# The last 65 keys of an attention kernel: queries become the stationary operand, VectorE turns the scores in blocks and ScalarE places them; the next x is read three groups later

## The chip, the cores and the metric

The kernel runs on one core of a Trainium2 chip. The time is the device time of one execution in microseconds (us). Before the change the median of three runs is 2532.07 us (2532.05 to 2533.65). The engines are PE (TensorE, with PEld for its weight loads), DVE (VectorE), ACT (ScalarE), POOL (GpSimd) and SP (SyncE, here only a DMA queue). A line such as L1246 is line 1246 of the kernel before the change.

## The reference

A gated cross-attention block followed by a mixture-of-experts layer, all in float32:

```python
# x (4, 256, 512), ctx_4096 (4, 1601, 512); 32 query heads, 8 key/value heads, head size 128
def attn(query, kv):                        # Wq (512, 4096), Wkv (512, 2048), Wo (4096, 512)
    q = (query @ Wq + bq).reshape(B, L, NKV, G, HDIM)            # G = 4 query heads share a key head
    k_, v_ = jnp.split(kv @ Wkv + bkv, 2, axis=-1)
    k, v = k_.reshape(B, Lk, NKV, HDIM), v_.reshape(B, Lk, NKV, HDIM)
    scores = jnp.einsum('blkgd,bmkd->bkglm', q, k) * scale
    a = jax.nn.softmax(scores, axis=-1)
    o = jnp.einsum('bkglm,bmkd->blkgd', a, v).reshape(B, L, NHEAD * HDIM)
    return o @ Wo + bo

x = x + tanh(g_xattn) * attn(layernorm(x), ctx_4096)
x = x + tanh(g_ffn) * moe(layernorm(x))     # a base matrix and 8 low-rank experts, the top 2 of them used
```

There are 1601 keys: twelve tiles of 128 and a rest of 65.

## The kernel before

**Groups.** Attention is done in 64 groups: 4 sequences `b`, 8 key heads `h`, 2 row blocks `l` of 128 queries. In one group the 4 query heads that share a key head lie side by side, so a group has W = 4 x 128 = 512 columns (query head, query). A group's scores are held with the keys on partitions: one tile `p` is 128 x 2 x 512, for a pair of key tiles. `pairs` begins with the rest alone (`(FULL,)`, unit j = 0), then six pairs of full tiles (j = 1 to 6).

**Scores** (`score_unit`, L1217 to L1261). For each key tile one float32 matmul: the keys `kT` (128 head dimensions x 128 keys, or x 65 for the rest) are the stationary operand, the 512 query columns of `qT` move, and the result lies in one PSUM bank with the keys on partitions. For the rest this is 65 partitions x 512. ScalarE copies the bank into the tile `p` (L1255). From unit j = 2 on, VectorE folds the tiles into a running maximum (`fold`, L1168 to L1181). The first fold, at j = 2, takes the pairs 1 and 2 and also the rest.

**Softmax and the second product.** `softmax` (L1268) finishes the maximum over the keys (five steps on VectorE, two of them block transposes), and queues for each unit a subtraction on VectorE (L1285), an exponential on ScalarE (L1288) and a sum on VectorE. `av_unit` (L1321 to L1337) multiplies with the values, `v` stationary. `run_group` (L1783) goes through the units of the current group and does the av units of the group before one step behind: scores j, then av j - 1. After a group `window` (L1800) puts in projections for the coming heads (q, k and v, in seven half-size products instead of eight, lines 1004 and 1015) and the output product (L472).

**What sets the order.** The instructions of TensorE, VectorE and ScalarE are issued in an order that a planner in the kernel's Python works out while it is traced. It keeps a clock for each engine: `spend(ns)` moves TensorE's clock on, `vec(ns)` and `act(ns)` those of VectorE and ScalarE, with durations that are written in the code. Work that may come later is put in queues (`later`), among them `sub`, `exp`, `ln` (layer norms), `sum` and `norm`. `pump` issues from the heads of the queues whatever can begin by the planner's clock, and in a tie the `sub` queue goes first. `fit("v", t)` issues queued work that fits before time `t`. `force(key)` issues a piece that is needed now. `Task`s hold TensorE steps with a due group. `short_tasks` (L1749) puts in steps of at most 432 ns between the units. On the chip each engine then runs its own instructions in this order and waits for semaphores. PSUM has 8 banks, given out by `bank` and given back by `give`.

**The next x.** Queries are projected for two sequences at once (`JOINT` = 2), so x is read twice: for sequences 0 and 1 at the start, for 2 and 3 in the middle. The second reading is started in the loop over groups, at (b, h, l) = (1, 4, 1), that is group 25, counting from 0:

```python
            if (h, l) == (NKV - 4, 1) and b + 1 < B and (b + 1) % JOINT == 0:
                load_pair("q", b + 1, 0)
                tasks.append(Task(x_steps(b + 1), now + 7))
```

`load_pair` issues on SP the load of the first query weights, kept in DRAM with their sums (896 KB). `x_steps` (L589) then issues: two loads of x tiles on SP (256 KB each), the bias `bo` on POOL; for each of four tiles a layer norm (VectorE statistics, a ScalarE square root, VectorE scaling), four transposes on TensorE with a VectorE copy out, a VectorE addition of the bias, two 128 KB stores on POOL and, for the first two, the load of one more tile on SP; at the end four VectorE differences (L653). The query projection of sequence 2, `pxq`, begins in the window after group (1, 7, 0) is scored, group 30.

Of the kernel before, what the change touches and what calls it, by code (L numbers as in the profile page):

```python
# [15 lines left out]
P = 128  # L16
NHEAD = 32
NKV = 8
HDIM = 128
G = NHEAD // NKV  # L20
# [7 lines left out]
def flamingo_kernel(  # L28
# [51 lines left out]
    nc = tc.nc  # L80
    B, L, D = x.shape
# [7 lines left out]
    FULL = KT - 1 if rows[-1] < P else KT  # L89
# [4 lines left out]
    pairs = [tuple(range(i, min(i + 2, FULL))) for i in range(0, FULL, 2)]  # L94
# [6 lines left out]
    HK = FULL // 2 * P  # L101
    NSUB = -(-HK // 512)
    SUB = HK // NSUB
    REST = rows[-1] if FULL < KT else 0
# [13 lines left out]
    SEM = 200  # L118
# [3 lines left out]
    clock = {"now": 0.0, "v": 0.0, "a": 0.0, "hold": 0.0}  # L122
    free = [0.0] * NBANK
    done = {}
    queues = {q: deque() for q in ("sub", "oT", "so", "exp", "ln", "T", "norm", "turn", "sum", "low", "low_a")}

    def vec(ns, ready=None):

        clock["v"] = max(clock["v"], clock["now"] + SEM if ready is None else ready) + ns
        return clock["v"] + SEM  # L130

    def act(ns, ready=None):
        clock["a"] = max(clock["a"], clock["now"] + SEM if ready is None else ready) + ns
        return clock["a"] + SEM
# [5 lines left out]
    def start_of(piece):  # L140
        engine, _, ready, _, _ = piece
        if not isinstance(ready, float):
            ready = done.get(ready, NEVER)
        return max(clock[engine], ready)

    def take(q):

        piece = q.popleft()
        engine, ns, _, fn, key = piece
        start = start_of(piece)  # L150
        fn()
        clock[engine] = start + ns
        if key is not None:
            done[key] = start + ns + SEM + (GP_COPIES if False else 0)

    def pump(until=NEVER, most=None):

        n = 0
        while most is None or n < most:
            heads = [(start_of(q[0]), i, q) for i, q in enumerate(queues.values()) if q]  # L160
            if not heads:
                return n
            start, _, q = min(heads)
            if start == NEVER or start + min(q[0][1], 1200) / 2 > until:
                return n
            take(q)
            n += 1
        return n
# [24 lines left out]
    def fit(engine, until):  # L193

        while True:
            some = [
                (start_of(q[0]), i, q)
                for i, q in enumerate(queues.values())
                if q and q[0][0] == engine and start_of(q[0]) + q[0][1] <= until + FIT
            ]  # L200
            if not some:
                return
            take(min(some)[2])

    def spend(ns, ready=0.0):

        clock["now"] = max(clock["now"], ready) + ns
        pump(clock["now"])
        turn_more()

    def bank(name):
        free.remove(min(free))
        return ps.tile([P, 512], F32, tag="bank", name=name)

    give = free.append
# [32 lines left out]
    def mm_cost(n):  # L248

        return 2 * (max(n, P) / 1.2 + 2)  # L250
# [126 lines left out]
    def by_blocks(b, h):  # L377
        return (b, h) not in heads[-2:]
# [206 lines left out]
    JOINT = 2  # L585
# [79 lines left out]
    def key_col(i):  # L665

        return HK if i == FULL else i * P + (REST if i * P >= HK else 0)
# [198 lines left out]
    qT_t, kT_t, v_t = {}, {}, {}  # L866
# [7 lines left out]
    def load_q(b, h):  # L874
        new_q(b, h)
        for g in range(0, G, 2):
            nc.sync.dma_start(qT_t[b, h][:, g : g + 2, :], q_kept[b, h, g])
# [339 lines left out]
    def score_unit(key, j):  # L1217

        b, h, l = key
        nm = "_".join(map(str, key))  # L1220
        free_p = 0.0
        if j == 0:
            p_t[key] = []
            acc_t[key] = pool.tile([P, 2, W], F32, tag="mx", name=f"mx_{nm}", bufs=1)
        if key == last and j > 0:

            if j == 1:
                flat = pool.tile([P, NC * 2 * HW], F32, tag="ctxT", name="p_last", bufs=1)
                late.extend(
                    flat[:, i * 2 * W : (i + 1) * 2 * W].rearrange("p (t w) -> p t w", t=2)  # L1230
                    for i in range(NPAIR - 1)
                )
            p = late.pop(0)
        else:

            if len(ring) >= NBUF:
                before, i = ring[-NBUF]
                free_p = force(("sum", before, max(i, min(NPAIR - FULL // 2 + 1, NPAIR - 1))))
            ring.append((key, j))
            p = pool.tile([P, 2, W], F32, tag="p", name=f"p_{nm}_{j}", bufs=NBUF)  # L1240
        p_t[key].append(p)
        for k, i in enumerate(pairs[j]):
            r = rows[i]
            spend(mm_cost(W), max(min(free), done.get(("qT", b, h), 0.0)))
            sc = bank(f"sc_{nm}_{i}")
            nc.tensor.matmul(  # L1246
                sc[:r, :],
                kT_t[b, h][:, key_col(i) : key_col(i) + r],
                qT_t[b, h][:, :, l * P : (l + 1) * P],
                start=True,  # L1250
                stop=True,
            )
            t = max(clock["now"] + SEM, free_p)
            fit("a", t)
            nc.scalar.copy(p[:r, k, :], sc[:r, :])  # L1255
            t = act(585, t)
            give(t)
        fit("v", t)
        ns = fold(acc_t[key], ALU.max, j, key)
        if ns:  # L1260
            vec(ns, t)  # L1261

    acc_t, sum_t, late, ring = {}, {}, [], []
    last = (B - 1, NKV - 1, NL - 1)
# [437 lines left out]
    tasks = []  # L1702
# [164 lines left out]
    def next_pair(b, hp):  # L1867
        return (b, hp + 1) if hp + 1 < NKV // 2 else (b + 1, 0) if b + 1 < B else None
# [107 lines left out]
    for hi, (b, h) in enumerate(heads):  # L1976
        pair, coming = (b, h // 2), next_pair(b, h // 2)
        nxt = heads[hi + 1] if hi + 1 < len(heads) else None
        for l in range(NL):
            now = hi * NL + l  # L1980
            cur = (b, h, l)
            if cur == last:
                break
            if (h, l) == (NKV - 4, 1) and b + 1 < B and (b + 1) % JOINT == 0:
                load_pair("q", b + 1, 0)
                tasks.append(Task(x_steps(b + 1), now + 7))
            swap_at["group"] = now
            run_group(cur, prev)
            if prev is not None:
                steps = out_steps(prev)  # L1990
                if steps:
                    tasks.insert(0, Task(steps, now + 1 if by_blocks(*prev[:2]) else None))
                    if by_blocks(*prev[:2]):
                        out_task[prev[:2]] = tasks[0]
            prev = cur
            if (b, h, l) == (B - 1, NKV - 3, NL - 1):
                tail_space()
                tasks.append(Task(ffn_weight_steps() + [(0, 0, early_norms)]))
                both = [ffn_steps(*t) for t in early]
                tasks[:0] = [Task(route, now + 4) for route, _ in both]  # L2000
                tasks.extend(Task(steps, spare=True) for _, steps in both)
            if nxt is not None and nxt[0] % JOINT == 0:
                tasks.append(Task(q_steps(*nxt, l), now, first=True))
            elif nxt is not None and l == 0:
                load_q(*nxt)
            if coming is not None and (h % 2, l) == (0, 1):
                cb, cp = coming
                if cb == b:
                    then = lambda c=coming: next_weights("v", *c)
                    steps = sum(pair_steps("k", cb, cp, then), [])  # L2010
                else:
                    steps = first_k_steps(cb)
                tasks.append(Task(steps, (hi | 1) * NL + (NL - 1) * (cb == b), now))
            if coming is not None and (h % 2, l) == (1, 0):
                cb, cp = coming
                follow = next_pair(cb, cp)
                then = None if follow is None else lambda f=follow: next_weights("k", *f)
                for part in pair_steps("v", cb, cp, then):
                    tasks.append(Task(part, (hi | 1) * NL + NL, now))
                if cb == b and cp == NKV // 2 - 1 and b + 1 < B:  # L2020
                    tasks.append(Task(ctx_steps(b + 1)))
            if (h, l) == (NKV - 1, NL - 1) and b + 1 < B:

                force(("T", "kv", b + 1))
                force(("w", "v", b + 1, 0))
            window(now)
            if l == NL - 1 and nxt == heads[-1]:
                load_wo(*nxt)
# [51 lines left out]
```

## Time and profile before

| | us |
|---|---|
| median of three runs | 2532.07 |
| the profiled execution | 2532.2 |
| its span, first to last instruction | 2530.4 |
| PE busy | 2521.6 |
| PEld busy | 1493.8 |
| DVE busy | 2175.3 |
| ACT busy | 1263.6 |
| POOL busy | 208.8 |

The TensorE clock granted in the records is 1.000 throughout. The largest groups of TensorE are the scores (L1246, 775.9 us in 1664 instructions) and the av products (L1337, 765.5 us in 1664). One float32 matmul is two instructions, each with its own weight load (LDWEIGHTS), so 13 key tiles x 64 groups x 2 make the 1664. ScalarE's copies of the scores (L1255) are 820 of 65 and 128 partitions in a mixed row, 586 ns each. A group takes 39.5 us on average (2530.4 / 64).

How to read the rows. A row of the groups has line, engine, operation, the tiles written and read, the shape and the count, then busy time in all and the mean duration of one in ns, then the idle time of the engine just before them. For a matmul the shape is stationary rows * columns, then the moving partitions x columns. Since TensorE overlaps its instructions, the duration of one is longer than the distance to the next: what an instruction takes from the engine is read from starts in the timeline. A row of the timeline has the start, the length of a run of like instructions, engine, line, tiles, shape and count. In a row of stretches (A:B) the columns are the stretch, its length, the busy time and in brackets the number of instructions, the granted clock, the share of the DMA engines and GB/s.

### The profile page before, as it was taken

Reading aid. Unit: us, or ns where it says so; the run is one execution under the profiler, and the core shown is the slowest. Engines: PE = TensorE matmul, PEld = TensorE weight load, DVE = VectorE, ACT = ScalarE, POOL = GpSimd, SP = SyncE. Lnnn points to the kernel's source line nnn. Section 1 sums busy time; section 2 is a strip of 40 time slices with the busy share of each in tenths; the row PEclk is TensorE's granted clock in tenths of the full one; section 3 lists DMA queues with packets and bytes.
Section 4 is the critical chain, followed back from the end, with each engine's and each line's share of the span. In section 5 each row is a group of like instructions: output and inputs, shape, how many; then the busy total and the mean of one; then the engine's idle time right before and its main releaser. Section 6 shows DMA issues by size and latency. Waiting matters only on the chain.

```text
span 2530.4 us, 27018 instructions
## 1 busy us (share of the span) xinstructions
PE 2521.6 (100%) x9199; PEld 1493.8 (59%) x9199; DVE 2175.3 (86%) x3323; ACT 1263.6 (50%) x2062; POOL 208.8 (8%) x271
## 2 busy tenths in 40 slices
PE   9999999999999999999999999999999999999999
PEld 7557566565555656555665565756656565555544
DVE  4999898898899989999878887878788888889886
ACT  2545454545455554555545454545455455555551
POOL 1000000001001000110010000000000100000100
PEclk9999999999999999999999999999999999999999
DMA  5646857669666543224255535455532222221211
GB/s 170 143 92 130 146 123 118 151 110 246 80 92 99 85 81 74 71 71 152 58 98 100 98 77 96 109 81 110 154 80 65 82 54 67 67 63 44 71 34 50
DMA packets 300136, 246.24 MB, mean 97 GB/s; under 512 B 180533, under 2 KB 256341, under 8 KB 296158
## 3 DMA queue, kind: packets, MB, share of 16 engines
q1 hardware_dynamic: 267278, 211.71, 36.6%
q0 software_dynamic: 32192, 32.55, 8.8%
q8 instruction: 72, 1.18, 0.2%
q14 instruction: 66, 0.54, 0.1%
q10 hardware_dynamic: 528, 0.26, 0.0%
HBM read 147.96 MB, written 96.49 MB: 97 GB/s over the span
## 4 chain that ended last, share of the span: by engine, by line
PE 98%; DVE 1%; DMA 0%; ACT 0%; issue 0%; SPq 0%; ACTq 0%
PE sc L1246 28%; PE av L1337 27%; PE pxv L1015 6%; PE pxk L1004 6%; PE pxq L1004 4%; PE pox L472 4%; PE pyv L1015 3%; PE pyk L1004 3%; PE pyq L1004 2%; PE poy L472 2%; PE pzv L1015 2%; PE pzk L1004 2%; PE pzq L1004 1%; PE ptv L1128 1%; PE poz L472 1%; PE py L1581 1%
## 5 line engine op out<-in xcount | busy, mean ns | idle before, releaser
L1246 PE MATMUL sc<-qT,kT 128*128 128x512 f32 (+1 forms) x1664 | 775.9, 592 | 0.0
L1337 PE MATMUL av<-p,v 65*128 65x512 f32 x1640 | 765.5, 592 | 0.5 <-ACT p L1288 0.5
L1255 ACT COPY p<-sc 65x512 f32<-65x512 f32 x820 | 478.4, 586 | 572.8 <-PE sc L1246 549.0
L1337 PEld LDWEIGHTS av<-p,v 65*128 65x128 f32 x1640 | 311.2, 190 | 384.3 <-issue 380.1
L1246 PEld LDWEIGHTS sc<-qT,kT 128*128 128x128 f32 (+1 forms) x1664 | 308.1, 186 | 375.6 <-issue 349.5
L1285 DVE TENSOR_TENSOR p<-p,mb 65x512 f32<-65x512 f32 x442 | 482.4, 1136 | 0.3
L1288 ACT ACTIVATE p<-p 65x512 f32<-65x512 f32 x442 | 422.3, 990 | 31.0 <-DVE p L1285 29.7
L1181 DVE TENSOR_TENSOR mx<-mx,p 128x1024 f32<-128x1024 f32 x252 | 308.1, 1223 | 146.3 <-ACT p L1255 141.7
L478 POOL DMA_DIRECT2D kept_x<-po x210 | 182.6, 925 | 2039.8 <-ACT po L477 1864.4
L1181 DVE TENSOR_TENSOR sm<-sm,p 128x1024 f32<-128x1024 f32 x252 | 307.6, 1221 | 42.0 <-ACT p L1288 32.0
L1004 PE MATMUL pxq<-xq,wq 128*128 128x256 f32 x512 | 131.2, 379 | 0.0
L1049 ACT ACTIVATE kT<-pxk,biasT 128x384 f32<-128x384 f32 (+1 forms) x120 | 58.1, 509 | 126.5 <-PE pxk L1004 126.0
L1004 PEld LDWEIGHTS pxq<-xq,wq 128*128 128x128 f32 x512 | 92.4, 189 | 32.1 <-issue 15.8
L1049 ACT ACTIVATE qT<-pxq,biasT 128x256 f32<-128x256 f32 x64 | 30.4, 474 | 148.8 <-PE pxq L1004 148.8
L1175 DVE TENSOR_TENSOR mx<-p,p 128x1024 f32<-128x1024 f32 x63 | 76.9, 1221 | 31.6 <-ACT p L1255 31.4
L1004 PE MATMUL pxk<-T,wk 128*128 128x417 f32 (+1 forms) x240 | 90.4, 499 | 0.0
L1015 PE MATMUL pxv<-wv,ctxT 128*128 128x128 f32 x720 | 90.2, 275 | 0.0
L1015 PE MATMUL pxv<-wv,T 128*128 128x128 f32 x720 | 90.2, 275 | 0.0
L1004 PE MATMUL pxk<-ctxT,wk 128*128 128x417 f32 (+1 forms) x240 | 90.0, 499 | 0.0
L1015 PEld LDWEIGHTS pxv<-wv,ctxT 128*128 128x128 f32 x720 | 86.4, 192 | 4.2 <-issue 3.8
L1015 PEld LDWEIGHTS pxv<-wv,T 128*128 128x128 f32 x720 | 86.4, 192 | 4.2 <-issue 3.8
L1052 ACT COPY v<-pxv 128x384 f32<-128x384 f32 x90 | 43.0, 478 | 83.4 <-PE pxv L1015 83.1
(273 smaller groups left out, 2779.5 us busy)
## 6 DMA issues: line engine op xcount, KB each, us to landing
kept_x<-po POOLq DMA_DIRECT2D x210, 128.0 KB, 4.8
wo<-kept_wo SPq DMA_DIRECT2D x22, 1024.0 KB, 7.8
kept_q<-wq SPq DMA_DIRECT2D x16, 896.0 KB, 4.3
wq<-kept_q SPq DMA_DIRECT2D x16, 896.0 KB, 5.1
space<-kept_wo SPq DMA_DIRECT2D x22, 512.0 KB, 3.9
wk<-kept_k SPq DMA_DIRECT2D x11, 896.0 KB, 4.8
wv<-kept_v SPq DMA_DIRECT2D x11, 896.0 KB, 4.6
ctxT<-kept_ctx SPq DMA_DIRECT2D x12, 801.0 KB, 11.8
```

Of the source, the lines that this page charges most:

```text
L472: nc.tensor.matmul(bk[:, :HD], left[i]()[:, c, :], blk[:, c, :], start=first and c == 0, stop=c == 1, skip_group_check=True,)
L478: nc.gpsimd.dma_start(x2_kept[b, l, d], part, accum_op=ALU.add)
L1004: nc.tensor.matmul(bk[:, :n], a(SLOT[i], c), operand(i, c, s, n), start=first and c == 0, stop=c == 1, skip_group_check=True,)
L1015: nc.tensor.matmul(bk[:, t * HDIM : (t + 1) * HDIM], operand(i, c, s + t * P, P), a(SLOT[i], c), start=first and t == 0 and c == 0, stop=c ...
L1049: nc.scalar.activation(dst, src, AF.Identity, bias=bias_of(kind, h0 + f))
L1175: nc.vector.tensor_tensor(acc, p[first], p[first + 1], op)
L1181: nc.vector.tensor_tensor(acc, acc, p[j], op)
L1246: nc.tensor.matmul(sc[:r, :], kT_t[b, h][:, key_col(i) : key_col(i) + r], qT_t[b, h][:, :, l * P : (l + 1) * P], start=True, stop=True,)
L1255: nc.scalar.copy(p[:r, k, :], sc[:r, :])
L1285: nc.vector.tensor_tensor(p, p, m, ALU.subtract)
L1288: nc.scalar.activation(p, p, AF.Exp, scale=scale)
L1337: nc.tensor.matmul(av, v_t[b, h][:r, i, :], p_t[key][j][:r, k, :], start=(j == 0 and k == 0), stop=(j == NPAIR - 1 and k == len(pairs[j]) ...
```

## The change

For the rest of 65 keys `score_unit` now calls a new function, `score_rest`. The 128 queries of each of the 4 query heads are the stationary operand (`qT`, 128 x 128), and the 65 keys move. This makes 4 float32 matmuls, side by side in one bank: queries on partitions, (query head, key) in 4 x 65 columns. VectorE then turns the result in blocks of 32 x 32, out of PSUM into the unused second half of the same tile `p`: one block transpose of 4 x 64 columns, and one of 4 x 32 columns in which the 65th key is repeated 32 times. A block transpose leaves each 32 x 32 block in its place among the partitions, so ScalarE moves the blocks to where they belong: 8 copies of 32 partitions x (4 x 32), and 4 copies of one partition x (4 x 32) for the 65th key. These 12 copies are issued in unit j = 1, behind the two copies of the first pair of full tiles, before the fold. The planner is told 8 x 62 ns for TensorE, 600 ns for VectorE and 12 x 220 ns for ScalarE, in place of 857 ns for TensorE and 585 ns for ScalarE.

The second reading of x starts at group (1, 6, 0), number 28, in place of 25, and is due 3 groups later in place of 7.

```diff
@@ score_unit @@
         p_t[key].append(p)
+        if pairs[j] == (FULL,):
+            score_rest(key, p, free_p)
+            return
         for k, i in enumerate(pairs[j]):
...
             nc.scalar.copy(p[:r, k, :], sc[:r, :])
             t = act(585, t)
             give(t)
+        if key in turned:
+            t = turned.pop(key)(t)
         fit("v", t)
...
+    turned = {}
+
+    def score_rest(key, p, free_p):
+
+        b, h, l = key
+        assert REST == 65
+        spend(G * 2 * 62, max(min(free), done.get(("qT", b, h), 0.0)))
+        sc = bank(f"sr_{'_'.join(map(str, key))}")
+        for g in range(G):
+            nc.tensor.matmul(
+                sc[:, g * REST : (g + 1) * REST],
+                qT_t[b, h][:, g, l * P : (l + 1) * P],
+                kT_t[b, h][:, HK : HK + REST],
+                start=True,
+                stop=True,
+            )
+        by_key = sc[:, : G * REST].rearrange("p (g k) -> p g k", k=REST)
+        two = p[:, 1, : 2 * P].rearrange("p (g k) -> p g k", k=64)
+        one = p[:, 1, 2 * P : 3 * P].rearrange("p (g k) -> p g k", k=32)
+        t = max(clock["now"] + SEM, free_p)
+        fit("v", t)
+        nc.vector.transpose(two, by_key[:, :, :64])
+        nc.vector.transpose(one, by_key[:, :, 64:65].to_broadcast([P, G, 32]))
+        give(vec(600, t))
+        t = clock["v"] + SEM
+
+        def place(after):
+            dst = p[:, 0, :].rearrange("p (g q) -> p g q", g=G)
+            for a in range(4):
+                q, k = slice(32 * a, 32 * a + 32), 32 * a
+                for c in range(2):
+                    nc.scalar.copy(dst[32 * c : 32 * c + 32, :, q], two[q, :, 32 * c : 32 * c + 32])
+                nc.scalar.copy(dst[64:65, :, q], one[k : k + 1])
+            return max(after, act(12 * 220, t))
+
+        turned[key] = place
...
@@ loop over the groups @@
-            if (h, l) == (NKV - 4, 1) and b + 1 < B and (b + 1) % JOINT == 0:
+            if (h, l) == (6, 0) and b + 1 < B and (b + 1) % JOINT == 0:
                 load_pair("q", b + 1, 0)
-                tasks.append(Task(x_steps(b + 1), now + 7))
+                tasks.append(Task(x_steps(b + 1), now + 3))
```

## The prediction

> **What bounds the kernel now.** I read the busy shares first, then the chain that ended last, then the groups with shapes kept apart (they separate the 65-key tile from the full ones), then stretches of the timeline for spacings, which the groups do not give.
>
> ```profile
> PE 2521.6 (100%) x9199; PEld 1493.8 (59%) x9199; DVE 2175.3 (86%) x3323; ACT 1263.6 (50%) x2062; POOL 208.8 (8%) x271
> PE 98%; DVE 1%; DMA 0%; ACT 0%; issue 0%; SPq 0%; ACTq 0%
> ```
>
> TensorE is the chain: 98% of it. Its own waits add up to 4.9 us in the table of waits. So a change gains only what it takes off TensorE's instruction stream and loses whatever makes TensorE wait; work on other engines is free as long as it stays hidden. Every matmul here is two instructions, each with a weight load of its own (9199 and 9199).
>
> The 65-key tile and what its replacement resembles, by shape, then as timeline rows (start, duration, count):
>
> ```profile
> L1246 PE MATMUL sc<-qT,kT 128*65 128x512 f32 x128 | 65.3, 592 | 0.0
> L1246 PEld LDWEIGHTS sc<-qT,kT 128*65 128x65 f32 x128 | 17.1, 137 | 7.9 <-issue 2.6
> L1015 PEld LDWEIGHTS pxv<-wv,ctxT 128*128 128x128 f32 x720 | 86.4, 192 | 4.2 <-issue 3.8
> ...
> 714.11 1.50 PE L1015 MATMUL pxv<-wv,T 128*128 128x128 f32 x12
> 715.45 1.50 PE L1015 MATMUL pyv<-wv,T 128*128 128x128 f32 x12
> ...
> 723.49 1.47 PE L1128 MATMUL ptv<-wv,rest 128*65 128x128 f32 x12
> 724.80 0.60 PE L1128 MATMUL ptv<-wv,T 128*65 128x128 f32 x4
> ...
> 1039.65 0.30 PEld L1004 LDWEIGHTS pyk<-T,wk 128*128 128x128 f32 x2 [1.16 <-ACT kT L1049]
> ...
> 2391.27 0.32 PEld L259 LDWEIGHTS pt_base<-ident,base 8*128 8x128 f32 x4 [0.76 <-issue]
> ```
>
> To be seen: (1) A load of 65 columns lasts 137 ns, one of 128 columns 192: 55 ns for 63 columns, so some 110 ns of a 128-column load go by columns. (2) With nothing streaming, two such loads start 0.30 - 0.19 = 0.11 us apart (1039.65). (3) Instructions with 128 moving and 128 stationary columns come 1.34 / 12 = 0.112 us apart (714.11 to 715.45); with 65 stationary columns 1.31 / 12 = 0.109 (723.49 to 724.80). The first is held by its load, the second by its stream. (4) Only transposes load 128 columns faster: (0.32 - 0.136) / 3 = 0.061 us apart.
>
> **The change, part by part.** There are 64 groups (4 sequences x 8 heads x 2 row blocks).
>
> *TensorE.* Removed per group: 2 instructions that stream 512 columns, 0.429 us apart (four of them take 1.72 us in the chain, read in order of time): 0.858 us. Added: 4 matmuls, so 8 instructions that stream 65 columns over 128 stationary ones. The stream shrinks to 65 x 0.429 / 512 = 0.054 us, but now each instruction brings a 128-column load, where the old tile loaded 65 columns twice under 0.429 us of stream. What bounds the new spacing: from below the transposes' 0.061 us, 8 x 0.061 = 0.49, a gain of 0.37 us a group, 23.7 us in all; from above a load that does not overlap the short stream, 0.107 + 0.054 = 0.161 us, 1.29 a group, a loss of 27 us. I take 0.112, because it is the one row with the same kind of instruction and the same load, and there load and stream already overlap (0.11 + 0.107 would be twice what is seen). 8 x 0.112 = 0.896: **+0.038 us a group, +2.4 us** in all; at 0.109 it is +0.9. The kernel's planner will charge 8 x 62 ns = 0.496, so it believes TensorE to be 0.4 us earlier per group than it is; what it places for ScalarE and VectorE then comes early rather than late for TensorE.
>
> On this spacing the Trainium skill holds two rules, both in "TensorE: Matmul & The Clock Gate". Section "LDWEIGHTS": a load costs its columns divided by 1.2, 107 ns for 128, which speaks against this change; as an estimate the tile would then cost 8 x 107 = 0.85 us, no gain. Section "Back-to-back issue gap": a matmul of 1 to 64 columns costs 25 ns or the 62 ns that its sequencer needs, which would make the tile 0.50 us and the kernel some 23 us faster. The rows at 714.11 and 1039.65 are of the first kind.
>
> *VectorE.* Added per group: a block transpose of 128x256 (the swap's, L718, 420 ns) and one of 128x128. The transposes of 128x512 take 711 ns, also out of PSUM (`tr<-su`, L1373), so 256 columns cost 291 and 128 columns about 275 ns. Together 0.70 us, 45 us in all, 86% to 88% busy. They lie beside TensorE. VectorE's in-order queue stands until TensorE has finished the tile; the subtractions and sums of the previous group are behind it, and their exponentials and the av matmuls wait for them.
>
> *ScalarE.* Removed: one 65x512 copy (581 ns). Added: 12 copies of up to 128 elements per partition. The two 128x128-sized copies L860 and L862 last 0.30 but start 0.21 us apart (6.14, 6.35), so a burst of 12 is 2.5 us: +1.9 us a group, 125 us in all, 50% to 55% busy. It stands behind the copies of the first pair of full tiles and waits for the two transposes. Behind it are the copies of the next pair, the exponentials of the previous group and the oT activation.
>
> The cover: how long before its av matmul an exponential is ready. I took it for all 64 groups from the timeline (end of the j-th L1288, start of the j-th av pair): by j, the median is 12 to 16 us and the tenth percentile 4.3 to 9.4. A 2.5 us burst is hidden in nearly all. The exceptions:
>
> ```profile
> 799.74 2.00 ACT L1288 ACTIVATE p<-p 128x1024 f32<-128x1024 f32 x2
> 801.63 1.45 PE L1337 MATMUL av<-p,v 128*128 128x512 f32 x3
> ...
> 1182.38 2.00 ACT L1288 ACTIVATE p<-p 128x1024 f32<-128x1024 f32 x2
> 1184.28 1.02 PE L1337 MATMUL av<-p,v 128*128 128x512 f32 x2
> ```
>
> The first of each two ends 0.8 us before its matmul; a third place (2410.7) has 1.3, and the last group none. Each can lose up to about the burst less the lead, 1.7 us, and a restart shows 0.1 us of weight load. Four places, 0 to 7 us; since the planner knows the burst and can shift it, I take **+1.5 us**. PSUM: the copies of the next pair come about 2.3 us late, with 8 banks of which av holds one; I cost that at nothing, and at one late pair per group (0.1 us) if the banks are held, 6 us.
>
> *The later x.* It moves from group 25 to 28 (1008 to 1117 us): on SP one 896 KB weight load and four 256 KB x loads, past the loads of wk (1150.9) and wv; on POOL one bias load and eight 128 KB stores of x, past the accumulating stores of kept_x; on ScalarE four square roots and the table loads around them (1.28 us each); on TensorE 16 transposes (1.7 us, only moved); on VectorE, from the groups, 4 x (0.69 + 0.18 + 0.15 + 0.15 + 0.55 + 0.69 + 0.74) + 4 x 0.68 = 15.3 us. Before, it took from 1008 to 1092 and its first user, pxq, came at 1201: a slack of 109 us, which is the move. Its new home, by stretch:
>
> ```profile
> core 0: us, DVE busy (x), PEclk, DMA share, GB/s
> 1008.40:1117.30 108.90, 101.36 (x152) 1.00 0.27 73
> 1117.30:1228.90 111.60, 104.21 (x150) 1.00 0.39 118
> ```
>
> There VectorE is idle for 7.4 us, and 15.3 must go in before 1201, beside the place at 1184 with its 0.8 us lead. Bounds: 0 if other VectorE work slips into the next group (11.5 us idle there), 15.3 - 7.4 = 8 us if it does not; below nothing by 1 us, as TensorE has two waits in the old home that may go (0.5 us of pyk at 1039.65, 0.6 of pox at 1099). I take **+2 us**, since subtractions go ahead of the x work in the planner's order.
>
> *Sum.* 2532.2 (the profiled execution: span 2530.4 and 1.8 around it) + 2.4 + 1.5 + 2.0 = 2538.1; the median of the runs is 2532.07, 0.1 less: **2538.0 us**, +0.23%. About 0.2% (5 us) is what a measurement of this kernel can tell from no change.
>
> **The rivals.** *A, nothing waits:* TensorE's own +0.9 to +2.4 us and full cover: 2533 to 2534.5, no change. For it: leads of 10 us and more almost everywhere. Against: the two crowded places above. *B, short loads:* the spacing is 0.061, as for transposes: 2532 - 23.7 + 3.5 = 2512, faster. It turns into a gain where the spacing falls below (0.858 - 3.5 / 64) / 8 = 0.100 us. For it: the planner's figure of 62 ns and the transposes. Against: no non-transpose instruction with a 128-column load comes closer than 0.108. *C, no overlap:* 0.161 us: 2532 + 27 + 3.5 = 2563. Against it: the 0.112 row. *D, ScalarE or VectorE becomes the bound in stretches:* in groups 15 to 30 VectorE is idle for only 1.2 to 5.7 us a group (busy time from one tile's start to the next), and the 0.7 us and the stand for TensorE use up the leads; one lost microsecond in each of those 16 groups and the 8 us of x give 2532 + 2.4 + 16 + 8 = 2558 at worst, 2545 in the middle. Against: those leads hold at some 10 us from group to group, so TensorE, not VectorE, sets the pace there.
>
> **How the numbers follow.** Forecast (TensorE +0.9 to 4, waits +1 to 6) 0.48; A 0.22; D 0.18; B 0.07; C 0.05. The forecast's own range is 2534 to 2542; 0.36 of its 0.48 lies above 2537.1, and 0.12 below. Slower: 0.36 + 0.18 + 0.05 = 0.59; same: 0.12 + 0.22 = 0.34; faster: B, 0.07. The range leaves out B, C and the far end of D: 2532 to 2555.
>
> **What the profile of the changed kernel would show.** The score matmuls of the tile as x512 instructions, about 0.112 us apart (8 in 0.90), at 0.06 if B holds, 0.16 if C. ScalarE's small copies x768, 0.21 apart; two transposes x64 of 0.42 and 0.28 us. TensorE's waits above 5 us in sum, the new ones near 800, 1184 to 1205 and 2410 us. Wrong it goes if the spacing is not the load's, or if the planner, with another clock, orders the projections otherwise and opens a wait that no row of before shows.

## The result and the profile after

The changed kernel takes **2551.27 us** (median of 5 runs, 2550.19 to 2555.08) against 2532.07 us before: a ratio of 1.0075, 95% interval 1.0064 to 1.0087. That is slower by 19 us, where the forecast was slower by 6 (2538.0, range 2532 to 2555). The profiled execution is the longest of the five, 2555.08 us with a span of 2551.7, so the rows below show about 2 us more than a middling one would. Rows are therefore weighed span against span: 2551.7 - 2530.4 = 21.3 us.

Busy shares and the shares of the chain that ended last, of the changed kernel's page:

```profile
PE 2531.1 (99%) x9583; PEld 1532.9 (60%) x9583; DVE 2207.6 (87%) x3451; ACT 1428.9 (56%) x2764; POOL 208.8 (8%) x271
PE 94%; DVE 4%; ACT 1%; DMA 1%; issue 0%; SPq 0%; DVEq 0%; ACTq 0%
```

TensorE still carries the chain, but 6% of it now lies on others, where it was 2%. ScalarE gained 165 us of busy time; 125 were forecast.

The groups of the new operations (columns as before: shapes and count, busy us and mean ns of one, idle us before them):

```profile
L1277 PE MATMUL sr<-kT,qT 128*128 128x65 f32 x512 | 64.1, 268 | 0.0
L1299 ACT COPY p<-p 32x128 f32<-32x128 f32 x512 | 151.4, 296 | 5.4 <-DVE p L1289 0.2
L1300 ACT COPY p<-p 1x128 f32<-1x128 f32 x256 | 75.4, 295 | 3.0
L1289 DVE STREAM_TRANSPOSE p<-sr 128x256 f32<-128x256 f32 x64 | 28.6, 446 | 22.8 <-PE sr L1277 22.4
L1290 DVE STREAM_TRANSPOSE p<-sr 128x128 f32<-128x128 f32 x64 | 17.5, 274 | 0.0
```

The two transposes take 0.72 us together, and VectorE stood 22.4 us for the tile in all, 0.35 us a group.

Two stretches of the timeline, first one tile on TensorE:

```profile
63.03 1.00 PE L1277 MATMUL sr<-kT,qT 128*128 128x65 f32 x8
63.86 1.51 PE L1249 MATMUL sc<-qT,kT 128*128 128x512 f32 x3
```

Then one burst of copies on ScalarE:

```profile
803.07 0.60 ACT L1299 COPY p<-p 32x128 f32<-32x128 f32 x2
803.68 0.29 ACT L1300 COPY p<-p 1x128 f32<-1x128 f32 x1
...
806.45 0.30 ACT L1300 COPY p<-p 1x128 f32<-1x128 f32 x1
806.75 1.06 ACT L1330 ACTIVATE p<-p 128x1024 f32<-128x1024 f32 x1
```

The tile's single starts in the trace are 0.112 us apart (the first follows its predecessor more closely, and the first full-tile matmul behind it starts its own successor 0.056 late); by them the tile takes 0.894 us, 0.891 to 0.896 in all 64 groups. The burst lasts 3.68 us (803.07 to 806.75), 0.307 a copy, where 2.5 was forecast.

TensorE's largest waits, from the table of waits (total us, times, longest us):

```profile
PE av L1379 <- ACT p L1330: 5.5, 2, 2.8
PE pox L472 <- DVE space L450: 3.9, 3, 2.3
PE po L1456 <- ACT oT L1441: 1.7, 1, 1.7
```

These three alone make 11.1 us; before, all waits were 4.9. The table does not show everything, though. A sharper measure is the distance between the starts of two matmuls, less what the first takes when nothing holds it (0.429 us for 512 columns, 0.216 for 256, 0.109 for 128 or less; the 0.056 us behind each new tile are counted with the tile). After the first 5 us this loss is 7.5 us before and **25.5 us** after. Three places make 14.2 of it: 4.6 at 1169 to 1182, 4.9 at 1189 to 1199, 4.7 at 2423 to 2431. The extra 18.0 us and the tile's 64 x (0.894 - 0.858) = 2.3 us are 20.3 of the span's 21.3.

The place at 1190, ScalarE's rows with TensorE's (timeline):

```profile
1189.64 1.05 ACT L1258 COPY p<-sc 128x512 f32<-128x512 f32 x2
1190.59 0.60 ACT L1299 COPY p<-p 32x128 f32<-32x128 f32 x2
1190.75 1.88 PE L1249 MATMUL sc<-qT,kT 128*128 128x512 f32 x4
...
1193.96 0.29 ACT L1300 COPY p<-p 1x128 f32<-1x128 f32 x1
1194.28 4.84 ACT L1330 ACTIVATE p<-p 128x1024 f32<-128x1024 f32 x5
...
1195.39 3.50 PE L1379 MATMUL av<-p,v 128*128 128x512 f32 x4 [2.76 <-ACT p L1330]
1198.69 0.81 PE L1249 MATMUL sc<-qT,kT 128*128 128x512 f32 x1
```

The burst runs from 1190.59 to 1194.28, and the exponential that TensorE needs stands behind it. The subtraction that the exponential needs was done by then (VectorE's row begins at 1188.68 and takes 1.2 us for one). So without the burst the exponential would have ended some 3.7 us earlier, at 1191.65, as an estimate; TensorE was done with its four score matmuls at 1190.75 + 1.72 = 1192.47. That is the lead of 0.8 us that the profile before showed here, less a burst of 3.69: 2.87 us of wait. The matmuls behind the wait are then slow as well: the row at 1195.39 covers four av instructions and 3.30 us to the next start, where four take 1.72.

That the clock is the reason shows in the same stretch, in the view by windows (stretch, length, PE busy, granted clock, DMA share, GB/s):

```profile
1160.00:1174.60 14.60, 14.47 (x37) 1.00 1.05 371
1175.00:1182.00 7.00, 4.67 (x10) 0.76 0.21 40
1182.00:1189.00 7.00, 7.00 (x31) 1.00 0.35 85
1189.00:1199.00 10.00, 7.24 (x13) 0.84 0.65 178
1199.00:1206.00 7.00, 7.00 (x19) 0.99 0.00 0
```

The granted clock falls only in the two stretches with a wait (the 0.99 in the last is the end of the second fall). The trace has it at exactly 0.5 from 1178.64 to 1182.06, from 1195.71 to 1199.12 and from 2427.92 to 2431.34 us, each time for 3.41 us. The 512-column matmuls there are 0.85 us apart, twice their 0.429. The three falls cost 1.68, 1.79 and 1.68 us over the waits, **5.2 us** in all. The profile before had a granted clock of 1.000 throughout.

### The profile page after: what moved, and what is told of

Its sections match the earlier page's. It is cut to its first block, busy times and chain, and to the rows that moved or that the text cites. A ratio compares the mean times of both kernels' runs of the same rounds, so it can differ in the third digit from the quotient of the medians.

```text
span 2551.7 us, 28563 instructions
## 1 busy us (share of the span) xinstructions
PE 2531.1 (99%) x9583; PEld 1532.9 (60%) x9583; DVE 2207.6 (87%) x3451; ACT 1428.9 (56%) x2764; POOL 208.8 (8%) x271
## 4 chain that ended last, share of the span: by engine, by line
PE 94%; DVE 4%; ACT 1%; DMA 1%; issue 0%; SPq 0%; DVEq 0%; ACTq 0%
PE av L1379 26%; PE sc L1249 24%; PE pxk L1004 6%; PE pxv L1015 6%; PE pxq L1004 4%; PE pox L472 4%; PE pyk L1004 3%; PE pyv L1015 3%; PE pyq L1004 2%; PE poy L472 2%; PE sr L1277 2%; PE pzk L1004 2%; PE pzv L1015 2%; PE pzq L1004 1%; PE ptv L1128 1%; PE poz L472 1%
## 5 line engine op out<-in xcount | busy, mean ns | idle before, releaser
L1249 PE MATMUL sc<-qT,kT 128*128 128x512 f32 x1536 | 725.0, 595 | 0.0
L1258 ACT COPY p<-sc 128x512 f32<-128x512 f32 x756 | 426.1, 587 | 414.9 <-PE sc L1249 380.7
L1249 PEld LDWEIGHTS sc<-qT,kT 128*128 128x128 f32 x1536 | 286.3, 190 | 332.9 <-issue 302.6
L1181 DVE TENSOR_TENSOR sm<-sm,p 128x1024 f32<-128x1024 f32 x252 | 307.1, 1219 | 14.2 <-ACT p L1330 3.4
L1299 ACT COPY p<-p 32x128 f32<-32x128 f32 x512 | 151.4, 296 | 5.4 <-DVE p L1289 0.2
L1175 DVE TENSOR_TENSOR sm<-p,p 128x1024 f32<-128x1024 f32 x63 | 76.5, 1214 | 15.9 <-ACT p L1330 15.2
```

What stands on the lines that cost most here:

```text
L1175: nc.vector.tensor_tensor(acc, p[first], p[first + 1], op)
L1181: nc.vector.tensor_tensor(acc, acc, p[j], op)
L1249: nc.tensor.matmul(sc[:r, :], kT_t[b, h][:, key_col(i) : key_col(i) + r], qT_t[b, h][:, :, l * P : (l + 1) * P], start=True, stop=True,)
L1299: nc.scalar.copy(dst[32 * c : 32 * c + 32, :, q], two[q, :, 32 * c : 32 * c + 32])
```

## The experiments

Times are medians; each ratio is against the kernel before on the same chip, where it took 2532.5 to 2532.8 us. "Loss" is TensorE's loss by starts as defined above (7.5 us before, 25.5 after).

**The x reading: undone in the changed kernel, and done alone.** In `e1_x_back` the new tile stays and x starts at group 25 again:

```diff
-            if (h, l) == (6, 0) and b + 1 < B and (b + 1) % JOINT == 0:
+            if (h, l) == (NKV - 4, 1) and b + 1 < B and (b + 1) % JOINT == 0:
...
-                tasks.append(Task(x_steps(b + 1), now + 3))
+                tasks.append(Task(x_steps(b + 1), now + 7))
```

> The changed kernel with the second reading of x put back to group 25, due in 7. In the changed kernel the waits of TensorE between 1168 and 1199 us, with the slow matmuls behind them, add up to about 9 us. Theory X (the move of x filled VectorE there): they vanish, 2542 us. Theory P (the burst of small copies on ScalarE is what the exponentials of group 29 come late behind, wherever x is): most of it stays, 2548 to 2553. The tile itself stays at 0.894 us in both.

`e2_x_only` is the kernel before with only the opposite edit.

> The kernel before with nothing changed but the second reading of x, at group 28 and due in 3. Theory X: the waits near 1170 to 1200 us come without the new tile, 2537 to 2541 us. Theory P: VectorE takes the 15.3 us without a wait above 1 us, 2531 to 2535.

Measured: `e2_x_only` 2533.57 us, ratio 1.0002 (0.9993 to 1.0012): alone, the later x changes nothing that can be told, as Theory P had it. `e1_x_back` 2562.66 us, ratio 1.0116 (1.0101 to 1.0131): 11.4 us *more* than the change, far above both expectations. With the new tile, the later x is not a cost; it avoids one.

Where `e1_x_back` loses it (timeline):

```profile
1106.76 1.88 PE L1249 MATMUL sc<-qT,kT 128*128 128x512 f32 x4
...
1107.60 1.42 DVE L653 TENSOR_TENSOR xq<-xq 128x512 f32<-128x512 f32 x2
...
1111.20 1.28 DVE L653 TENSOR_TENSOR xq<-xq 128x512 f32<-128x512 f32 x2
1111.37 1.07 ACT L1258 COPY p<-sc 128x512 f32<-128x512 f32 x2 [2.53 <-DVE sm L1181]
...
1114.36 0.69 DVE L1438 TENSOR_TENSOR oT<-av,rb 128x512 f32<-128x512 f32 x1
...
1116.10 0.42 DVE L450 TENSOR_TENSOR space<-oT 128x256 f32<-128x256 f32 x1
...
1117.03 1.22 PE L472 MATMUL pox<-space,space 128*128 128x256 f32 x2 [8.39 <-DVE space L450]
```

From 1100.7 to 1117 VectorE works without a gap, and the oT product and the differences that `pox` needs (L1438, L450) stand behind maxima, sums and the x work. TensorE waits 8.4 us and then loses 3.1 more at half clock. ScalarE's copies of the scores wait for VectorE too. By loss, the stretch from 1097 to 1123 takes 14.1 us with the earlier x; the two places in x's new home, 1169 to 1199, take 9.5 in the change. Another 2.9 us are a `pxq` wait at 322 us. It is not the x reading's doing: up to about 1025 us both kernels issue the same instructions in the same order on every engine, so this is a difference between two executions. 14.1 - 9.5 + 2.9 = 7.5 answers to the spans, 2558.9 - 2551.7 = 7.2. The traces thus show 4.6 us for the x reading; the 11.4 us between the medians carry some 5 us of uncertainty from the intervals.

**The burst: two copies in place of twelve.** `e3_one_copy` moves the same tile with 2 copies, so the scores of the rest are not put where they belong:

```diff
-            for a in range(4):
...
-            return max(after, act(12 * 220, t))
+            nc.scalar.copy(p[:REST, 0, : 3 * P], p[:REST, 1, : 3 * P])
+            nc.scalar.copy(p[:REST, 0, 3 * P :], p[:REST, 1, :P])
+            return max(after, act(700, t))
```

> The changed kernel with two copies of 65 rows (384 and 128 columns) in place of the 12 that move the blocks, charged 700 ns to ScalarE by the planner: the scores of the rest then stand in wrong places, so the placing is left out, all else stays. Theory P: the waits near 1192 and 2423 us, where the exponentials came late behind the burst, go with it, -8 to -12 us, 2539 to 2543. Theory X: only what stands at 2423 goes, 2545 to 2548. In neither does the tile change (0.894 us).

Measured: 2541.69 us, ratio 1.0036 (1.0023 to 1.0049), 9.6 us less than the change. The two copies last 511 and 296 ns. Loss 13.2 us; the places at 745 to 820, 1169 to 1182 and 2424 are gone, the one at 1197 has shrunk to 1.0 us, and no clock falls. Its largest wait, in the table of waits, was 0.4 us in the change:

```profile
PE pxq L1004 <- DVE qs_q L1059: 4.0, 3, 2.1
```

This is inside Theory P's 2539 to 2543. So the burst is a cause, and with the order that goes with it about half of the 19 us; without it some 9 us stay, of which the tile accounts for 2.3. One thing is not separated: the planner is also told 700 ns in place of 2640, so the order changes too. A run with the order kept and only the copies gone was not made. The `pxq` waits may be in part a difference between executions, as the one at 322 us was in `e1_x_back`.

**What the planner is told.** `e4_true_x_back` gives the measured durations, with x at group 25 as in `e1_x_back`; `e4c_pe_true` keeps the change but for TensorE's figure (112); `e6_copy_pe_true` is `e3_one_copy` with that one edit.

```diff
-        spend(G * 2 * 62, max(min(free), done.get(("qT", b, h), 0.0)))
+        spend(G * 2 * 112, max(min(free), done.get(("qT", b, h), 0.0)))
...
-        give(vec(600, t))
+        give(vec(700, t))
...
-            return max(after, act(12 * 220, t))
+            return max(after, act(12 * 307, t))
```

> The same as e1_x_back, and the planner told what the profile shows: 8 x 112 ns for the tile on TensorE, 700 ns for the two transposes, 12 x 307 ns for the copies. Theory C (the planner's wrong figures open the waits, 3.68 us of burst where it reckons with 2.64): TensorE's waits fall by half or more against e1_x_back, 2536 to 2539. If the burst costs whatever the planner knows: within 2 us of e1_x_back.

> The changed kernel, x where the change puts it, and the planner told 8 x 112 ns for the tile in place of 8 x 62, nothing else. If the planner's TensorE clock is what opens the waits: 2540 to 2546. If it is the burst, which it still reckons at 2.64 us: 2549 to 2553.

> The two copies of e3_one_copy in place of the burst (the placing left out again) and the planner told 8 x 112 ns for the tile. If burst and false clock are all that the change costs beside the tile: 2534 to 2537, the tile's 2.3 us and up to 2.5 of waits. If something else waits (the transposes on VectorE): 2538 to 2542, as e3_one_copy.

Measured: `e4_true_x_back` 2548.94 us, ratio 1.0061 (1.0046 to 1.0076), 13.7 less than `e1_x_back`, which is neither of its two expectations. `e4c_pe_true` 2545.08, ratio 1.0046 (1.0030 to 1.0063), 6.2 less than the change and in the range for the planner's clock. `e6_copy_pe_true` 2536.40 in 10 runs, ratio 1.0017 (1.0008 to 1.0026), 5.3 less than `e3_one_copy` and in its first range. The operations on the chip are the same with 62 and 112, but for two table loads on ScalarE; their order differs. What is left of two of the change's waits in `e4c_pe_true`, where the burst is still there:

```profile
PE av L1379 <- ACT p L1330: 4.6, 3, 1.8
PE pox L472 <- DVE space L450: 2.0, 1, 2.0
```

The `pox` wait here is a new one, at 179 us; the three of the change, at 745, 818 and 1177 us, are gone. The clock falls once and not three times, which is worth 3.4 us. Four kernels make a table:

| TensorE's figure in the planner | 12 copies | 2 copies | difference |
|---|---|---|---|
| 8 x 62 ns | 2551.27 (the change) | 2541.69 | 9.6 |
| 8 x 112 ns | 2545.08 | 2536.40 | 8.7 |
| difference | 6.2 | 5.3 | |

From 2532.7 to 2551.3: the burst, with the planner told of it, 8.7 to 9.6 us, the figure of 62 ns 5.3 to 6.2, and 3.7 for what stays in `e6_copy_pe_true`, 2.3 of it the tile. Each difference carries some 4 to 5 us of uncertainty from the intervals. The figure's effect is thus only just clear of it, and that the rows and columns agree in size says only that the two add, roughly.

**True figures with x in other places.** `e7_true_51` and `e7_true_60` have all three measured durations; x starts at (5, 1), due 4 groups later, and at (6, 0), due 2 groups later.

> The whole change with all three figures of the planner as in e4_true_x_back, and x read from group (1, 5, 1) on, due in 4. The tile's 2.3 us are a floor of 2534. If knowing the true costs is enough: 2537 to 2543, better than the change (2551) and e4c_pe_true (2545). If 3.7 us of burst find no room: 2545 to 2550.

> The same with x where the change puts it, (1, 6, 0), due in 2. 2537 to 2543 if the true costs are enough; 2545 to 2552 if x and burst meet at 1170 to 1200 us as in the change.

Measured: 2544.95 us, ratio 1.0050 (1.0035 to 1.0065), and 2552.82, ratio 1.0076 (1.0060 to 1.0093). Both missed the range for true costs being enough. The second has three true figures and is not faster than the change with its wrong ones; but its x is also due in 2 groups in place of 3, and the three figures with x exactly as in the change were not run. Its table of waits has one of 3.0 us of the x transposes for the layer norm, which the change's table does not have.

```profile
PE av L1379 <- ACT p L1330: 6.1, 3, 2.8
PE pt_x L259 <- DVE xn L284: 3.0, 1, 3.0
PE pxq L1004 <- DVE qs_q L1059: 2.6, 3, 1.7
```

True figures did not make this order good. 2545 us is the best that the whole change reached; no version beat the kernel before.

**The copies on GpSimd.** `e5_pool` gives the 12 copies to the engine that was 8% busy:

```diff
-                    nc.scalar.copy(dst[32 * c : 32 * c + 32, :, q], two[q, :, 32 * c : 32 * c + 32])
-                nc.scalar.copy(dst[64:65, :, q], one[k : k + 1])
-            return max(after, act(12 * 220, t))
+                    nc.gpsimd.tensor_copy(dst[32 * c : 32 * c + 32, :, q], two[q, :, 32 * c : 32 * c + 32])
+                nc.gpsimd.tensor_copy(dst[64:65, :, q], one[k : k + 1])
+            return max(after, t + 12 * 400)
```

> The changed kernel with the 12 copies on GpSimd instead of ScalarE (the planner told of 12 x 400 ns and of no ScalarE time). If the burst on ScalarE holds up the exponentials and oT: as with two copies in its place, 2540 to 2544, or more where GpSimd is slower than 400 ns a copy or its DMA issues stand behind the copies. If the burst's cost is a matter of the order alone: 2550.

Measured: 2598.28 us, ratio 1.0264 (1.0249 to 1.0280). Two of its groups say why:

```profile
L1299 POOL COPY p<-p 32x128 f32<-32x128 f32 x512 | 275.2, 538 | 127.5 <-DVE p L1289 76.0 <-ACT kT L1049 31.0
L1178 DVE TENSOR_TENSOR mx<-mx,p 65x512 f32<-65x512 f32 x64 | 44.0, 688 | 140.6 <-POOL p L1300 140.1
```

A copy lasts 538 ns there, and GpSimd's queue also stands for other engines. VectorE then waits 140 us for the tile before its fold, 2.2 us a group, with all its queue behind.

**What sets the spacing of small matmuls.** `p1_shapes` is the change with four further matmuls per group in heads 1, 2 and 3 of every four, whose result nothing uses:

```diff
+        n_m, n_s = ((65, 128), (33, 128), (128, 128), (65, 64))[h % 4]
...
+                    qT_t[b, h][:, g, l * P : l * P + n_s],
+                    kT_t[b, h][:, HK - 64 : HK - 64 + n_m],
```

> The changed kernel with a second set of four matmuls behind the tile in three heads of four, in a bank of its own and used for nothing: 33 moving columns over 128 stationary, 128 over 128, and 65 over 64. If the column count of the load sets the spacing: 0.112 us apart with 33 and with 128 moving columns alike, and about 0.06 with 64 stationary ones. If the moving columns set it: about 0.06, 0.109 and 0.06. The time of the whole is of no interest here (some 40 us of TensorE more).

Measured (its single time, 2591.9 us, holds the added work): three rows of the timeline, stationary rows * columns, then moving:

```profile
128.74 1.03 PE L1288 MATMUL ex<-kT,qT 128*128 128x33 f32 x8
...
211.84 1.11 PE L1288 MATMUL ex<-kT,qT 128*128 128x128 f32 x8
...
298.78 0.68 PE L1288 MATMUL ex<-kT,qT 128*64 128x65 f32 x8
```

Single starts are 0.112 us apart with 33 moving columns and with 128, and **0.058** with 64 stationary columns. The stationary columns set the spacing: turning the operands round swapped a stream that hid a load for a load that nothing hides. The Trainium skill, "TensorE: Matmul & The Clock Gate", section "LDWEIGHTS", has a load at its columns divided by 1.2, so 107 and 53 ns; these rows agree to within 5 ns. The same page's section "Back-to-back issue gap" has 25 or 62 ns for 1 to 64 moving columns, but as the gap of isolated matmuls; for a stream of loads and matmuls it says that both set the spacing. As a price for the new tile, which is how the prediction quoted it, the 25 or 62 ns do not fit: 33 columns came at 112.

**Lone copies, and how long a wait costs the clock.** `p2_copies_stalls` is the kernel before with 8 spare copies after each of the groups 46 to 53, one form per group, and after groups 32 to 43 a TensorE step that waits for a chain of 1 to 6 spare ScalarE copies.

```diff
+            if 32 <= now < 44:
+                stall(1 + now % 6, now)
+            if 46 <= now < 54:
+                copies(now - 46)
```

> The kernel before with eight ScalarE copies of 128 elements behind each of the groups 46 to 53, of one kind a group (128 partitions; 32; 32 to other partitions; within a tile; within a tile to other partitions; one partition; 64 elements), and with TensorE made to wait for a chain of 1 to 6 ScalarE copies after groups 32 to 43, twice each length. Copies: 0.21 us apart where they overlap as L860 and L862 did, 0.31 in the kinds that do not; theory D (a copy that reads and writes the same tile does not overlap with the next) has 0.31 in the two kinds within a tile alone, theory M (the move to other partitions) in the two kinds that move. Waits: if a wait of TensorE halves its clock from some length on, the 512-column instructions behind it come 0.853 us apart for some 3 us, in none of the waits below 1.5 us and in most of those above 2.5.

Measured (one run, 2559.07 us with the added work): all six 128-element forms are 0.33 us apart, whether 128, 32 or one partition, moved or not; the 64-element forms 0.275. Both theories of the copies fell: neither the move between partitions nor the partition count explains 0.307 against 0.21. But all eight copies of a form wrote one place, which the next run takes apart. The waits were 0.85 to 2.50 us. Of the two of 2.50 the one at 1424 us halved the clock, the one at 1686 did not, by windows:

```profile
1424.48:1427.90 3.42, 1.09 (x7) 1.00 0.06 11
1427.90:1431.31 3.41, 3.41 (x10) 0.50 0.22 67
1431.31:1434.72 3.41, 3.41 (x17) 1.00 0.00 0
1683.90:1687.31 3.41, 2.15 (x6) 1.00 0.07 2
1687.31:1690.73 3.42, 2.35 (x12) 1.00 0.27 79
```

The first cost 1.7 us behind the wait. The other, and all shorter ones, cost 0.06 at most. The windows shown lie on a grid that all fourteen traces keep: the granted clock changes only at whole multiples of 3.41 us after its first step to 1.00. The first wait falls into one such stretch, which leaves TensorE 1.09 us of work in it; the second is cut in two by the grid.

`p3_copies` is the kernel before with 8 spare 64-element copies per form, two destinations in turn:

```diff
+            ((a, scr[:32, :64]), (a, scr[:32, 64:])),
+            ((a, scr[:32, :64]), (b, scr[32:64, :64])),
```

> The kernel before with eight ScalarE copies of 64 elements behind each of the groups 46 to 51, in two alternating forms a group: to two halves of the columns on the same partitions; to the same columns on other partitions; to interleaved columns; all to the same place; to other columns on other partitions; each reading what the one before wrote. Theory W (a copy waits for the end of the one before only where the columns that the two write overlap, whatever the partitions): 0.275 us apart in the second, third and fourth group, some 0.15 to 0.18 in the first and the fifth. Theory S (every copy from SBUF to SBUF of this kind waits for the end of the one before): 0.275 in all six.

Measured (one run, 2531.95 us). The two forms of the diff, in order, from the timeline:

```profile
1857.80 1.26 ACT L1988 COPY scr<-ident 32x64 f32<-32x64 f32 x8
...
1901.55 2.12 ACT L1988 COPY scr<-ident 32x64 f32<-32x64 f32 x8
```

Other columns on the same partitions: 0.146 us apart, so a copy begins before the one ahead of it ends. Other partitions: 0.268. Interleaved columns of the same partitions also come at 0.146; the same place over again, other partitions with other columns, and a copy that reads what the last one wrote at 0.268 to 0.275. Both theories as written fell on one form or the other. What fits all six is that two copies overlap only if the second writes other columns of the same partitions and doesn't read what the first wrote. Every copy of the change's burst goes to other partitions than the one before. The rows L860 and L862, from which 0.21 was taken, write other columns of the same partitions. That the same 12 copies, sorted by destination, would run faster was not tried.

## Why the prediction was right and wrong

The sign and the range held, and the size did not: +19 us against +6. The range held by luck in part: the forecast's own range ended at 2542, and the stated one reached 2555 only because it took in most of rival D, which came about otherwise than written (below). By its steps:

- *TensorE's tile, 8 x 0.112 = 0.896, +2.4 us.* Right: 0.894, +2.3 us. Rivals B (0.061) and C (0.161) fell with it, and the shapes run showed why. The bound from the transposes was no bound for this kind of instruction.
- *VectorE, 0.70 us, its queue standing for the tile.* Right: 0.72, and 22.4 us of standing.
- *ScalarE's burst of 2.5 us.* Mis-sized: 3.68, because 0.21 was the spacing of copies that overlap. The price was read from the nearest row by size, and it was the wrong row by destination.
- *Four places of short lead, +1.5 us, at most 7.* The mechanism was right and two of the places were named (1184 and 2410, now 1195 and 2427). They measured 2.9 us of wait each by starts. The step's own formula, burst less lead, gives 3.68 - 0.8 = 2.9 and 3.68 - 1.3 = 2.4 with the true burst. At 800 no av matmul waited, and the last group lost nothing new. Of the six versions with the twelve copies on ScalarE, all have an av wait between 2423 and 2460 us, of 1.9 to 2.9 us, and five have one near 1190 (not `e1_x_back`); with two copies, in both versions, nothing above 0.4 us waits in the first of these stretches, and at most 1.0 in the second.
- *A restart costs 0.1 us of weight load.* Wrong, and one of the largest holes: behind three waits the clock was halved, 5.2 us. Nothing in the profile before had a wait long enough to show it. The Trainium skill's "TensorE: Matmul & The Clock Gate", section "Why this matters for your kernels", asks for no idle gaps above about 3 us; the measurement decides, and here gaps of 2.5 to 2.9 us were enough, and in two other runs 2.05.
- *The planner with 62 ns places work early rather than late, which was taken as harmless.* Wrong: it costs 5.3 to 6.2 us, give or take 4 to 5. In the change it shows in the `pox` waits and in two of the three falls of the clock, which are gone with 112. Why the order made with 62 opens them is not shown; the runs show that the order made with 112 loses less (17.6 us against 25.5 with twelve copies, 11.4 against 13.2 with two), and that the burst and this error roughly add.
- *The later x, +2 us, 0 to 8.* Wrong: alone +0.8 (within the measurement's uncertainty), within the change a saving of 11.4 by the medians, of which the traces show 4.6 at the x reading.
- *Waits that the prediction did not name:* `pox` at 1177.5 (2.5 us, then the clock), at 818 (1.7) and at 745 (0.5), all for L450; and 2.6 us around `su` and `po` near the end, where the trace before had 0.3. The first three are gone without the burst (`e3_one_copy`), but also with the burst and the figure of 112 (`e4c_pe_true`). So in these runs they came only with the burst and the order made with 62 together. That ScalarE's late copies hold up VectorE's maxima, and those the oT product ahead of L450, is read from the order of the rows and was not tried by itself.
- *D, VectorE the bound in stretches, 2545 to 2558.* The time lies in its range, the mechanism mostly not: not one microsecond in each of 16 groups, but three places of 4.6 to 4.9. In the place at 1177.5 VectorE is indeed full (6.90 of 7.00 us busy, from 1175).

The sum with measured terms, for the profiled execution: tile 2.3, the three places 14.2, the other waits 3.8 (18.0 - 14.2, net of waits of before that are gone), 20.3 of 21.3 us.

What stays open: why 62 in place of 112 makes a worse order, and what a planner with true figures would need in order to keep TensorE fed in x's home.

## What to carry to other kernels

Price a burst of small copies by a row with the same pattern of destinations, and then go through the places of shortest lead with "burst less lead", since an average cover of 10 us says nothing about the two places that have 0.8. Add to any wait of 2 us or more on TensorE another 1.7 us for the clock, as a cost that may or may not come: it came where about 2 us of standing fell into one 3.41 us stretch of the clock's grid. Where an order is worked out from durations written in code, a wrong duration is itself a change to be measured: change it alone, and expect an order that improves in one place and not everywhere.

## What the hardware showed that was not expected

- Waits from 2.05 us on TensorE can halve its clock for 3.41 us, at some 1.7 us each. It is not certain: in `p2_copies_stalls` one of two equal waits of 2.50 us did it, in `e4c_pe_true` one of 2.15 and in `e7_true_51` one of 2.05 did, in `e1_x_back` one of 2.84 did not.
- The traces also show when. Cut each of the fourteen into stretches of 3.41 us from the first step to a clock of 1.00, and leave out the start: at full clock, all 18 stretches in which TensorE was busy for at most 1.42 us were followed by a halved one, and none in which it was busy for 1.56 us or more; of the four between, three were. A wait that the grid cuts in two can pass.
- ScalarE copies of 64 elements within SBUF come 0.146 us apart into other columns of the same partitions, and 0.268 into other partitions or when they depend on the one before. In the change, 128 elements into alternating partitions came at 0.307.
- A float32 matmul's two instructions each came at the pace of their weight load: 0.112 us for 128 stationary columns, with 33, 65 or 128 columns moving, and 0.058 for 64 with 65 moving.
- GpSimd takes 538 ns on average for a copy of 32 x 128 that takes ScalarE 296.
